# A Restormer block on one core: bands of 16 rows instead of 12, the fourth channel block of every band split by rows between VectorE and TensorE, one pool of sixteen buffers, and an order read from a table of places

## The chip, the core and the metric

The kernel runs on one core of one Trainium2 chip. The metric is device time in microseconds (us), the median of several runs. The core's engines work side by side, each on its own queue of instructions in program order: TensorE (PE, with its weight loads as PEld), VectorE (DVE), ScalarE (ACT), GpSimd (POOL) and SyncE (SP, which only issues transfers). Sixteen DMA engines move data for all of them. An engine that reaches an instruction whose operands are not there waits, and everything behind it on that queue waits too.

## The reference

The input is 16 images of 128 channels and 96x96 pixels, f32. Of each image:

```python
xn1 = _layernorm(x_hwc, ln1_w, ln1_b)            # over the 128 channels of a pixel
attn_out = _attention(xn1, wq, wk, wv, wp)       # 8 heads; channels attend to channels, 16 x 16 a head
x = x + attn_out.transpose(0, 3, 1, 2)
xn2 = _layernorm(x_hwc, ln2_w, ln2_b).transpose(0, 3, 1, 2)
x = x + _ffn(xn2, w_in, w_dw, w_out)
# _ffn: h1 = 1x1 convolution 128 -> 512; h2 = depthwise 3x3 of h1, padding 1;
#       h3 = gelu(h2); 1x1 convolution 512 -> 128
```

## The kernel before

The 128 channels lie on the partitions. An image goes through a first normalisation (names with `_a`), a gram matrix and the attention, which end in one 128x128 matrix for the image (`mats`); then that matrix times the normalised pixels is added to x (`mix`, `mixed`, `add_x`), a second normalisation (names with `_b`) writes the ring `xn`, and the feed-forward part reads the ring. The normalisation of the next image runs beside the convolutions of this one. In a normalisation PE transposes four tiles of 128 pixels into a bank of PSUM, DVE takes statistics (`BATCH_NORM_STATS2`, L876), POOL makes the reciprocal root (L881, L885) and, in the first normalisation, scales the pixels (L909).

The feed-forward part is cut into bands of `BR = 12` rows and four blocks of 128 hidden channels (`NCH = 4`). A band and a block are one job (`conv_job`):

1. `hidden` (PE, L1162) makes the hidden rows in PSUM, 4 or 5 at a time, and `kept` (ACT, L1167) copies them into the padded tile `h1s[n]`. The two rows that a band shares with the one before are copied by `halo` (ACT, L1158).
2. Of the nine taps of the depthwise convolution, ACT multiplies two, three or four out (`product`, L1178, into tiles `pr`). Weights are divided by that of the centre tap, so that the centre needs no product.
3. POOL adds the first product to the centre tap (`merge`, L1181, into the one tile `merged`) and, where there is a fourth product, adds that (`merge_too`, L1184).
4. DVE adds the other taps one after another (`tap`): the first reads `merged` and writes the accumulator `acc` in PSUM (L1190), the middle ones add into `acc` (L1194), the last writes the job's tile `h3` (L1190 again, `h<-h,ratio,acc`). Each of them needs the one before.
5. Transfers issued by POOL add the rest: `add_products` (L1203) the third product into the second, `add_h3` (L1206) the second into `h3`. `gelu` (ACT, L1211) then works in place on `h3`.

The fourth block (`PE_CHUNK`) of a third of the bands (`PE_BANDS`: 10 of every 30, and others in the last image) is instead convolved by PE itself (`by_matmuls`, L1274: nine matmuls for each unit of `UR = 4` rows, and one for the edges, L1280). When the four blocks of a band are done, `ffn_out` multiplies them unit by unit with the output weights (PE, L1315), DVE adds the result to x (L1322), and SP stores the band.

The buffers are pools of their own: `XB_BUFS = 5` bands of x, `PR_BUFS = 8` products, `H3_BUFS = 8` tiles of h3, one `merged`, all of 12 rows, and `X1_BUFS = 2` bands of x for the first normalisation. Four banks of PSUM (`H_BANKS`) serve all that PE writes outside `acc` and the gram matrix.

The order of all this is made by `Plan`: every piece of work is given an engine, a duration, a place (`AT`, `RANK`, and `SHIFTS` for each stretch of the work), its reads and its writes. `Plan.order` plays the engines through in time with these durations: an engine that is free takes the ready work with the lowest place. It also books the time in which POOL and DVE may not read two SBUF tiles at once (`two`, `held`). The program is emitted in the order of the starts that come out.

Of the kernel before, what the change touches and what calls it, by code (L numbers as in the profile page):

```python
# [18 lines left out]
BR = 12  # L19
PE_CHUNK = 3  # L20
PE_BANDS = (0, 3, 6, 9, 12, 15, 18, 21, 24, 27)
PE_OF = 30
PE_LAST = (0, 1, 3, 4, 6)
# [8 lines left out]
FOURTHS = ((0, 1, (0,)),)  # L32
FOURTH_TAP = 6
LAST_TAP, TOP_LAST, END_LAST = 8, 6, 2
RING = 132
# [7 lines left out]
X1_BUFS = 2  # L43
XB_BUFS = 5
PR_BUFS = 8
H3_BUFS = 8
ZT_BUFS = 4
BATCHES = 8
DIRECT = False
IN_TURN = ("zT", "tr", "h3", "pr", "xb", "x1")  # L50
AT = dict(
    load_w=-385.3, weights=-616.15, zeros=-141.7, load_a=-42.4, forth_a=-588.2, stats_a=1671.35, variance_a=269.75,
    power_a=-755.3, pool_product=152.05, merge=-380.8, scaled_a=-1419.9, gram=1191.75, back_a=416.05,
    place_a=228.35, attention=-37, mix=1454.35, residual=-779.15, mixed=-33.8, add_x=-342.3, forth_b=1585.15,
    stats_b=614.45, variance_b=-1160.25, power_b=-1398.6, shift_b=20.9, scaled_b=-3615.05, back_b=417.3,
    place_b=-902.15, halo=4531.85, hidden=416.95, kept=-903.15, products=3487.6, add_last=-380.1, tap=10.85,
    add_first=-1420.85, gelu=4569.5, conv=1192.9, conv_gelu=10.15, out=421.1, add=612.75, store=75.2,
    mix_0=-440.15, residual_0=-785.8, mixed_0=-1036.75, add_x_0=-1518.55, gram_0=475.45, forth_a_0=-103.4,
    forth_b_0=-946.85, stats_a_0=-789.15, stats_b_0=-710.05, scaled_a_0=-915.5, copied_a=35.4, copied_b=-38.35,
    copied_a_0=-43.45, copied_b_0=1111, scaled_b_0=-128.2, back_a_0=485, back_b_0=-1340.55, place_a_0=-547.95,  # L60
    place_b_0=-708.95, shift_b_0=22.8, late=-293.55, load_a_0=-390.35, load_dw=-378, units=-654.05,
    variance_a_0=-172.3, power_a_0=-183.6, variance_b_0=-303.2, power_b_0=-128.75,
)
RANK = dict(tap=-1882.15, products=-1879.1, forth_a=-433, forth_b=-526, conv_gelu=-1389, mix=-1794.75)
STRETCH = 15
SHIFTS = {
    0: dict(load_w=1.9, zeros=-8.4, load_a=-22.8, forth_a=-1.1, stats_a=-0.3, variance_a=-0.3, power_a=-8.1,
        merge=-300.7, gram=0.2, back_a=-0.2, place_a=-1660.1, attention=-276.4, mix=-21.7, residual=-23.2,
        mixed=530.5, forth_b=40.5, stats_b=-118.7, variance_b=14.1, power_b=605.1, back_b=0.1, place_b=1.6,
        halo=4.3, kept=986.6, products=-7.1, add_last=329.8, tap=-1.6, add_first=1.7, gelu=7.1, conv=-6,  # L70
        conv_gelu=0.4, out=0.2, add=-660.9, store=1.7, mix_0=-899, residual_0=-622, gram_0=0.9, forth_a_0=18.5,
        stats_a_0=-2.4, stats_b_0=19.6, scaled_a_0=-65.5, copied_a=-60.9, back_a_0=-6.5, back_b_0=0.2,
        place_a_0=399.7, place_b_0=1296.2, late=10.6, load_a_0=4.4, load_dw=229.6, units=8.6, variance_a_0=619.5,
        power_a_0=-469.8, variance_b_0=-341, power_b_0=-17.1),
    1: dict(load_a=-14.5, forth_a=0.1, stats_a=14.8, variance_a=1354, power_a=1176.9, merge=637, scaled_a=46.3,
# [124 lines left out]
    31: dict(merge=4987, hidden=741.3, kept=1.8, products=1119.8, tap=1184.1, add_first=2628.9, gelu=-4553.7,  # L200
        conv=9, conv_gelu=-2.6, out=4185.8, add=-1517.3, store=4532.1),
}
STEP = dict(scaled=0.3, hidden=0.1, products=0.5, tap=0.166, conv=1.6, conv_tap=0.03, out=0.8, out_part=0.05)
SLACK = 150
LATE = 400
NORM1_END = 6.0
# [1193 lines left out]
```

## Time and profile before

| what | value |
|---|---|
| median of 3 runs | 3966.26 us (3965.86 to 3970.24) |
| span of the profiled execution | 3974.3 us, 0.2% above the median; no other time of it is given |
| PE busy | 3892.4 us, 98% of the span |
| DVE busy | 3834.8 us, 96% |
| ACT busy | 3558.1 us, 90% |
| POOL busy | 3379.4 us, 85% |
| DMA moved | 777.42 MB, 196 GB/s over the span |

The busy time of an engine is the time in which at least one of its instructions is under way; an instruction can begin a little before the one ahead of it ends, so busy time is less than the sum of the durations. In a group of instructions the numbers behind the bar are the busy time in us, the mean of one in ns, and the idle time of the engine just ahead of them with what ended most of it. Rows of the timeline give the start and the length of a run of equal instructions, both in us.

### The profile page before, as it was taken

The page shows a single profiled execution, that of the slowest core. Times are in us where ns is not written, and L with a number is a line of the kernel's source. Part 1 is how long each engine was busy: PE and PEld are TensorE (multiplying, and loading weights), DVE is VectorE, ACT ScalarE, POOL GpSimd, SP SyncE. Part 2 cuts the span into 40 slices and gives each one's busy share as a digit, 9 for nine tenths or more (in the row PEclk, how much of TensorE's full clock was granted, in tenths as well). Part 3 has the DMA queues.
Part 4 walks back from the last instruction along what each step waited for, and adds up shares of the span by engine and source line. Part 5 has one row for each costly group of instructions (what it writes and reads, how often), then busy time and mean ns, then how long its engine had stood idle before and what let it go on. Part 6 is the DMA issues. An engine that isn't in the chain of part 4 may idle for free.

```text
span 3974.3 us, 50973 instructions
## 1 busy us (share of the span) xinstructions
PE 3892.4 (98%) x16760; PEld 2521.7 (63%) x16760; DVE 3834.8 (96%) x4390; ACT 3558.1 (90%) x5186; POOL 3379.4 (85%) x3107
## 2 busy tenths in 40 slices
PE   8999999999999999999999999999999999999999
PEld 7566666666666666666666666666666666665555
DVE  7999999999999999999999999999999999999998
ACT  3989989989999999999989989999899999998886
POOL 5998988898898988988888888888888888888674
PEclk9999999999999999999999999999999999999999
DMA  3999999999999999999999999999999999999996
GB/s 100 187 191 204 200 200 198 199 202 198 210 201 209 203 198 203 200 210 201 194 202 197 207 201 194 205 197 206 189 192 206 203 207 201 203 197 183 191 189 146
DMA packets 191691, 777.42 MB, mean 196 GB/s; under 512 B 22208, under 2 KB 23616, under 8 KB 191424
## 3 DMA queue, kind: packets, MB, share of 16 engines
q0 software_dynamic: 151920, 622.33, 82.6%
q1 hardware_dynamic: 38784, 151.75, 10.2%
q8 instruction: 132, 2.16, 0.2%
q14 instruction: 135, 1.11, 0.1%
q10 hardware_dynamic: 720, 0.07, 0.0%
HBM read 148.85 MB, written 75.50 MB: 56 GB/s over the span
## 4 chain that ended last, share of the span: by engine, by line
PE 58%; DVE 14%; ACT 10%; DMA 7%; POOL 6%; issue 5%; POOLq 0%; DVEq 0%; ACTq 0%
PE h L1315 15%; PE h L1162 14%; PE h L1274 13%; DVE acc L1194 6%; DMA h<-pr 5%; ACT pr L1178 5%; PE h L818 4%; PE h L964 4%; PE g L916 3%; PE h L868 3%; DVE acc L1190 3%; DVE h L1190 2%; ACT h L1167 2%; POOL merged L1181 2%; DMA pr<-pr 2%
## 5 line engine op out<-in xcount | busy, mean ns | idle before, releaser
L1178 ACT ACTIVATE pr<-h,ratio 128x1152 f32<-128x1152 f32 x1494 | 1837.2, 1271 | 37.6 <-DMA h<-pr 12.6
L1194 DVE SCALAR_TENSOR_TENSOR acc<-h,ratio,acc 128x1152 f32<-128x1152 f32 (+1 forms) x1308 | 1810.3, 1384 | 7.7
L1181 POOL TENSOR_TENSOR merged<-pr,h 128x1152 f32<-128x1152 f32 x466 | 1238.1, 2657 | 100.5 <-DVE acc L1190 54.7
L1162 PE MATMUL h<-xn,winT 128*128 128x384 f32 (+2 forms) x2802 | 1088.0, 496 | 16.0 <-ACT h L1167 9.2
L1315 PE MATMUL h<-h,woutT 128*128 128x384 f32 x3072 | 1086.2, 488 | 1.7 <-ACT h L1167 1.1
L1274 PE MATMUL h<-xn,comp 128*128 128x380 f32 (+2 forms) x2430 | 895.0, 482 | 2.2 <-ACT h L1167 1.5
L1167 ACT COPY h<-h 128x384 f32<-128x384 f32 (+2 forms) x1401 | 652.9, 493 | 192.4 <-PE h L1162 187.5
L1315 PEld LDWEIGHTS h<-h,woutT 128*128 128x128 f32 x3072 | 565.2, 190 | 359.3 <-ACT h L1167 7.8
L1162 PEld LDWEIGHTS h<-xn,winT 128*128 128x128 f32 x2802 | 500.0, 190 | 326.6 <-issue 34.2
L1190 DVE SCALAR_TENSOR_TENSOR acc<-h,ratio,merged 128x1152 f32<-128x1152 f32 x466 | 686.6, 1473 | 20.9 <-POOL merged L1184 10.1
L1206 POOL DMA_DIRECT2D h<-pr x466 | 463.3, 994 | 241.9 <-DVE h L1190 57.5
L1190 DVE SCALAR_TENSOR_TENSOR h<-h,ratio,acc 128x1152 f32<-128x1152 f32 x467 | 655.2, 1403 | 3.4
L1211 ACT ACTIVATE h<-h,ksum 128x1152 f32<-128x1152 f32 (+2 forms) x586 | 616.0, 1081 | 46.4 <-DMA h<-pr 45.6
L1274 PEld LDWEIGHTS h<-xn,comp 128*128 128x128 f32 x2430 | 430.6, 189 | 235.2 <-issue 17.1
L1203 POOL DMA_DIRECT2D pr<-pr x466 | 478.7, 1040 | 103.1 <-ACT pr L1178 73.4
L885 POOL TENSOR_TENSOR ve_b<-ve_b,mhalf 128x4 f32<-128x4 f32 x288 | 366.0, 1277 | 7.9
L909 POOL TENSOR_TENSOR zT<-zT,ve_a 128x512 f32<-128x512 f32 x270 | 331.3, 1232 | 8.6
L885 POOL TENSOR_TENSOR ve_a<-ve_a,mhalf 128x4 f32<-128x4 f32 x288 | 318.6, 1109 | 15.3
L868 PE MATMUL h<-ident,x 128*128 128x128 f32 x2244 | 317.0, 275 | 13.7 <-ACT xn L970 4.9
L868 PEld LDWEIGHTS h<-ident,x 128*128 128x128 f32 x2244 | 263.6, 142 | 96.4 <-issue 38.6
L818 PE MATMUL h<-xn,mwT 128*128 128x384 f32 x768 | 289.1, 490 | 7.7 <-ACT h L1167 3.2
L916 PEld LDWEIGHTS g<-zT 128*128 128x128 f32 x2160 | 269.9, 191 | 40.2 <-POOL zT L909 11.0
(190 smaller groups left out, 3967.0 us busy)
## 6 DMA issues: line engine op xcount, KB each, us to landing
pr<-pr POOLq DMA_DIRECT2D x466, 576.0 KB, 7.8
h<-pr POOLq DMA_DIRECT2D x466, 576.0 KB, 7.7
x<-in_x_dram SPq DMA_DIRECT2D x128, 576.0 KB, 7.5
out_dram<-x SPq DMA_DIRECT2D x127, 576.0 KB, 4.6
x<-in_x_dram POOLq DMA_DIRECT2D x123, 576.0 KB, 9.1
out_dram<-x SPq DMA_DIRECT2D x3, 192.0 KB, 1.9
h<-in_L_conv_w_in_dram SPq DMA_DIRECT2D x1, 256.0 KB, 3.4
h<-in_L_conv_w_out_dram SPq DMA_DIRECT2D x1, 256.0 KB, 3.6
```

The costliest lines, as they stand in the source:

```text
L868: nc.tensor.transpose(d["pT", q][:, k, :], xt[:, j * P : (j + 1) * P], ident)
L885: nc.gpsimd.tensor_tensor(rstd, rstd, mhalf, ALU.pow)
L1162: nc.tensor.matmul(rows(ph), lhsT=winT[:, n, :], rhs=window(xn, r0 + r, e - r, 1), start=True, stop=True)
L1167: nc.scalar.copy(window(h1_, r, e - r, 1), rows(d.pop(("ph", r))))
L1178: nc.scalar.activation(to, shifted(t), AF.Copy, scale=ratio[:, n, t : t + 1])
L1181: nc.gpsimd.tensor_tensor(merged, d["pr", dma_taps[0]], shifted(UNIT), ALU.add)
L1190: nc.vector.scalar_tensor_tensor(to, shifted(t), ratio[:, n, t : t + 1], also, ALU.mult, ALU.add)
L1194: nc.vector.scalar_tensor_tensor(to, shifted(t)[:, lo:hi, cut], ratio[:, n, t : t + 1], to, ALU.mult, ALU.add)
L1203: nc.gpsimd.dma_start(out=d["pr", dma_taps[1]], in_=d["pr", t], accum_op=ALU.add)
L1211: nc.scalar.activation(h3, h3, AF.Gelu, bias=ksum[:, z, n : n + 1])
L1274: nc.tensor.matmul(d["pc"][:, lo:hi, cut], lhsT=comp[:, t, :], rhs=window(xn, r0 + dy, UR, dx)[:, lo:hi, cut], start=(t == order[0]), stop ...
L1315: nc.tensor.matmul(rows(d["po"]), lhsT=woutT[:, n, :], rhs=h3s[g, n][:, s * UR : (s + 1) * UR, :], start=(k == 0), stop=(k == NCH - 1),)
```

## The change

- `BR` becomes 16: six bands an image instead of eight, 24 jobs an image instead of about 29. A whole tap is 128x1536 instead of 128x1152, and `acc` fills its three banks.
- The fourth block of every band is split: PE convolves the last unit of 4 rows of the band (`PE_UNITS = 1`; two or three units in the bands of the last image, `PE_LAST`), and a job of the remaining 12 rows goes the way of the other blocks. That job makes all its hidden rows itself and has no `halo`.
- A fourth product is taken in blocks 0 and 2 of every band and in block 1 of every second one (`FOURTHS`), but not in the first and the last band of an image; before only in block 0.
- `merge` adds in place into the product's own tile; the tile `merged` is gone.
- x, products and h3 share `BUFS = 16` tiles of 16 rows. The first normalisation loads x in pieces of `XR = 8` rows into three small tiles.
- `ffn_out` works on `OC = 512` columns instead of 384: three pieces a band, each with an add and, in the last band, a store.
- `Plan.op` takes neither engine nor duration. Each piece of work has a place from the table `PLACES`: one for the first image, one that is repeated for images 1 to 14 with `PERIOD` added for each, one for the last. `Plan.order` emits the ready work with the lowest place for which a buffer is free; nothing is played through in time, and `two` and `held` are gone.

```diff
-BR = 12
+BR = 16
+XR = 8
+OC = 512
 PE_CHUNK = 3
-PE_BANDS = (0, 3, 6, 9, 12, 15, 18, 21, 24, 27)
-PE_OF = 30
-PE_LAST = (0, 1, 3, 4, 6)
+PE_UNITS = 1
+PE_LAST = (2, 2, 2, 2, 2, 3)
...
-FOURTHS = ((0, 1, (0,)),)
+FOURTHS = ((0, 1, (0,)), (2, 1, (0,)), (1, 2, (0,)))
...
-X1_BUFS = 2
-XB_BUFS = 5
-PR_BUFS = 8
-H3_BUFS = 8
-ZT_BUFS = 4
+X1_BUFS = 3
+XB_FIRST = 4
+BUFS = 16
+ZT_BUFS = 3
...
+PERIOD = 2533.91
+PLACES = (
...
+        tap=(862.03, 886.3, 688.92, 919.54, 935.53, 955.22, 974.9, 995.58, 1012.83, 1030.39, 1045.8, 1136.89,
...
 class Plan:
...
+        if kind:
+            n = self.count[kind] = self.count.get(kind, -1) + 1
+            self.place = self.at + PLACES[self.era][kind][n]
+        self.ops.append((self.place, list(needs), new, work))
...
+        while ready:
+            place, k = heapq.heappop(ready)
+            new = ops[k][2]
+            pools = [t[0] for t in new]
+            lacks = [p for p in pools if len(free[p]) < pools.count(p)]
+            if lacks:
+                waiting[lacks[0]].append(k)
+                continue
+            for t in new:
+                self.slot[t] = free[t[0]].pop(0)
+            order.append(k)
...
-    merged = h1p.tile([P, BR, W], F32, name="merged")
-    pr_bufs = [h1p.tile([P, BR, W], F32, name=f"pr_{k}") for k in range(PR_BUFS)]
-    h3_bufs = [h1p.tile([P, BR, W], F32, name=f"h3_{k}") for k in range(H3_BUFS)]
+    bufs = [h1p.tile([P, BR, W], F32, name=f"buf_{k}") for k in range(BUFS)]
...
     def conv_job(j, g, n):
...
-        from_halo = b > 0 and (n != PE_CHUNK or not by_pe(g - 1))
-        to_halo = b < NB - 1 and (n != PE_CHUNK or not by_pe(g + 1))
+        R = BR if n != PE_CHUNK else BR - UR * pe_units(g)
+        whole = R == BR
+        top, bottom = b == 0, b == NB - 1 and whole
+        from_halo, to_halo = b > 0 and whole, b < NB - 1 and whole
...
         def merge():
-            nc.gpsimd.tensor_tensor(merged, d["pr", dma_taps[0]], shifted(UNIT), ALU.add)
+            nc.gpsimd.tensor_tensor(d["pr", dma_taps[0]], d["pr", dma_taps[0]], shifted(UNIT), ALU.add)
 
         def merge_too():
-            nc.gpsimd.tensor_tensor(merged, merged, d["pr", dma_taps[3]], ALU.add)
+            nc.gpsimd.tensor_tensor(d["pr", dma_taps[0]], d["pr", dma_taps[0]], d["pr", dma_taps[3]], ALU.add)
...
-    def ffn_out(p, g, s):
+    def ffn_out(g, s):
...
             nc.tensor.matmul(
-                rows(d["po"]), lhsT=woutT[:, n, :], rhs=h3s[g, n][:, s * UR : (s + 1) * UR, :],
-                start=(k == 0), stop=(k == NCH - 1),
+                d["po"], lhsT=woutT[:, n, :], rhs=flat(h3s[g, n])[:, cols], start=(k == 0), stop=(k == NCH - 1)
             )
...
+    def pe_units(g):
+        i, b = divmod(g, NB)
+        return PE_LAST[b] if i == B - 1 else PE_UNITS
```

The order on DVE, in the middle of the program (the second job of a band). In the names `h_0_141` to `h_3_144` are the padded hidden tiles of the four blocks before, and `h_0_157` to `h_3_160` those after, `h_73` to `h_76` the four banks, `zT` the transposed pixels, `buf` the common tiles. Before:

```order
L1190 SCALAR_TENSOR_TENSOR acc<-h_1_142,ratio,merged 128x1152
L876 BN_STATS st_a_5_13366<-zT_162 128x6
L1194 SCALAR_TENSOR_TENSOR acc<-h_1_142,ratio,acc 128x1056
L968 TENSOR_TENSOR xn<-x_8_0_13009,h_76 128x4x96
L1194 SCALAR_TENSOR_TENSOR acc<-h_1_142,ratio,acc 128x1056
L968 TENSOR_TENSOR xn<-x_8_1_13223,h_73 128x4x96
L1194 SCALAR_TENSOR_TENSOR acc<-h_1_142,ratio,acc 128x1056
L968 TENSOR_TENSOR xn<-x_8_1_13223,h_74 128x4x96
L1190 SCALAR_TENSOR_TENSOR h_2_156<-h_1_142,ratio,acc 128x1152
```

And the same engine after, about the middle of its program too (the end of a band and the first job of the next):

```order
L1275 SCALAR_TENSOR_TENSOR acc<-h_3_160,ratio,acc 128x1152
L1271 SCALAR_TENSOR_TENSOR buf_169<-h_3_160,ratio,acc 128x1152
L1271 SCALAR_TENSOR_TENSOR acc<-h_0_157,ratio,buf_162 128x1536
L1275 SCALAR_TENSOR_TENSOR acc<-h_0_157,ratio,acc 128x1536 x2
L1271 SCALAR_TENSOR_TENSOR buf_167<-h_0_157,ratio,acc 128x1536
L948 BN_STATS st_137<-zT_178 128x6 x2
L1271 SCALAR_TENSOR_TENSOR acc<-h_1_158,ratio,buf_166 128x1536
L1275 SCALAR_TENSOR_TENSOR acc<-h_1_158,ratio,acc 128x1536
```

Before, almost every tap has another piece of work between itself and the next tap; after, several taps follow each other directly. Counted over the whole program, a tap stands directly ahead of another tap 374 times among 2,258 before, and 801 times among 1,780 after.

The order on POOL, in the middle of the program: the merges, what stands right behind them, and the issues of the transfers. Before:

```order
L1206 DMA h_1_155<-pr_148 128x1152
L1203 DMA pr_153<-pr_151 128x1152
L1181 TENSOR_TENSOR merged<-pr_146,h_1_142 128x1152
L1206 DMA h_2_156<-pr_147 128x1152
L1203 DMA pr_149<-pr_152 128x1152
L1181 TENSOR_TENSOR merged<-pr_150,h_2_143 128x1152
L881 TENSOR_SCALAR ve_b_2_10268<-st_b_2_10237 128x4
```

After:

```order
L1283 DMA buf_172<-buf_174 128x1536
L1280 DMA buf_171<-buf_161 128x1152
L953 TENSOR_SCALAR ve_140<-st_132 128x4
L957 TENSOR_TENSOR ve_140<-ve_140,mhalf 128x4
L1262 TENSOR_TENSOR buf_168<-buf_168,h_0_157 128x1536
L1265 TENSOR_TENSOR buf_168<-buf_168,buf_169 128x1536
L953 TENSOR_SCALAR ve_145<-st_137 128x4
L1280 DMA buf_176<-buf_170 128x1536
```

Every merge had the tile `merged` as its goal, so that it stood behind the first tap of the job before; now each goes into a tile of its own, and merges of two additions are more frequent (160 second additions among 383 jobs with merges, against 96 among 466). The last merge of a job has a short instruction or an issue behind it nearly everywhere, before and after: another long addition or scaling follows directly 31 times in 464 before and 2 times in 382 after.

911 lines of the change are left out of this document (428 added, 483 removed), and 125 rows, old and new, of tables (conv, hidden, kept, out).

## The prediction

> **What bounds the kernel now.** I read the first part of the page, then the busy time by stretch, then the groups with different shapes apart, then short pieces of the timeline, because on queues this full the step from one start to the next says more than a duration.
>
> ```profile
> span 3974.3 us, 50973 instructions
> ...
> PE 3892.4 (98%) x16760; PEld 2521.7 (63%) x16760; DVE 3834.8 (96%) x4390; ACT 3558.1 (90%) x5186; POOL 3379.4 (85%) x3107
> ...
> DMA packets 191691, 777.42 MB, mean 196 GB/s; under 512 B 22208, under 2 KB 23616, under 8 KB 191424
> ...
> q0 software_dynamic: 151920, 622.33, 82.6%
> q1 hardware_dynamic: 38784, 151.75, 10.2%
> ```
>
> Five resources are nearly full. The stretches (busy us of PE, PEld, DVE, ACT, POOL, then the granted clock, the DMA share and GB/s) say where the idle time lies:
>
> ```profile
> 0.00:100.00 100.00, 90.02 (x596) 73.11 (x597) 72.50 (x186) 35.01 (x73) 55.83 (x113) 1.00 0.34 101
> 700.00:1200.00 500.00, 495.30 (x2172) 322.88 (x2171) 491.05 (x558) 463.74 (x682) 440.42 (x403) 1.00 0.97 203
> 3450.00:3500.00 50.00, 47.37 (x208) 30.58 (x207) 47.11 (x55) 45.56 (x66) 43.53 (x43) 1.00 1.04 224
> 3900.00:3975.00 75.00, 70.77 (x229) 41.50 (x227) 58.80 (x51) 38.75 (x54) 25.33 (x18) 0.99 0.60 132
> ```
>
> In the body PE and DVE are both busy 98 to 99%, ACT 93%, POOL 88%. So PE and DVE bound the kernel together: a gain on one alone is worth nothing. Of the 139.5 us that DVE idles, 27.5 lie in the first 100 us and 16.2 in the last 75; the body holds 95.8, or 2.5%.
>
> **The change, engine by engine.** Instructions and elements are counted from both programs; durations and steps come from these rows.
>
> ```profile
> L1178 ACT ACTIVATE pr<-h,ratio 128x1152 f32<-128x1152 f32 x1494 | 1837.2, 1271 | 37.6 <-DMA h<-pr 12.6 <-DMA pr<-pr 10.0 <-POOL merged L1181 2.2
> L1194 DVE SCALAR_TENSOR_TENSOR acc<-h,ratio,acc 128x1152 f32<-128x1152 f32 x957 | 1349.9, 1411 | 5.3
> L1181 POOL TENSOR_TENSOR merged<-pr,h 128x1152 f32<-128x1152 f32 x466 | 1238.1, 2657 | 100.5 <-DVE acc L1190 54.7 <-ACT pr L1178 28.6 <-ACT h L1167 5.1
> L1315 PE MATMUL h<-h,woutT 128*128 128x384 f32 x3072 | 1086.2, 488 | 1.7 <-ACT h L1167 1.1 <-ACT h L1211 0.2
> L1190 DVE SCALAR_TENSOR_TENSOR acc<-h,ratio,merged 128x1152 f32<-128x1152 f32 x466 | 686.6, 1473 | 20.9 <-POOL merged L1184 10.1 <-POOL merged L1181 4.2 <-DVE h L1190 0.5
> L1190 DVE SCALAR_TENSOR_TENSOR h<-h,ratio,acc 128x1152 f32<-128x1152 f32 x467 | 655.2, 1403 | 3.4
> L1167 ACT COPY h<-h 128x384 f32<-128x384 f32 x1092 | 506.8, 488 | 144.8 <-PE h L1162 142.0
> L1203 POOL DMA_DIRECT2D pr<-pr x466 | 478.7, 1040 | 103.1 <-ACT pr L1178 73.4 <-ACT h L1158 11.0 <-ACT x L827 3.6
> L1194 DVE SCALAR_TENSOR_TENSOR acc<-h,ratio,acc 128x1056 f32<-128x1056 f32 x351 | 460.4, 1312 | 2.3
> L909 POOL TENSOR_TENSOR zT<-zT,ve_a 128x512 f32<-128x512 f32 x270 | 331.3, 1232 | 8.6
> L1322 DVE TENSOR_TENSOR x<-h,x 128x384 f32<-128x384 f32 x384 | 211.6, 551 | 39.3 <-PE h L1315 31.6 <-ACT pr L1178 3.2 <-issue 1.7
> L1167 ACT COPY h<-h 128x480 f32<-128x480 f32 x192 | 105.7, 566 | 33.5 <-PE h L1162 31.6 <-DVE xn L968 1.5
> L1280 PE MATMUL h<-ident,edgeT 6*128 6x8 f32 x248 | 47.6, 262 | 0.0
> ```
>
> ```profile
> 1510.79 1.40 DVE L1194 SCALAR_TENSOR_TENSOR acc<-h,ratio,acc 128x1152 f32<-128x1152 f32 x1
> 1512.10 0.42 DVE L876 BATCH_NORM_STATS2 st_a<-zT 128x6 f32<-128x256 f32 x1
> 1512.44 2.86 DVE L1194 SCALAR_TENSOR_TENSOR acc<-h,ratio,acc 128x1152 f32<-128x1152 f32 x2
> ```
>
> ```profile
> 1513.45 4.03 PE L1315 MATMUL h<-h,woutT 128*128 128x384 f32 x12
> ```
>
> ```profile
> 1514.08 3.55 ACT L1178 ACTIVATE pr<-h,ratio 128x1152 f32<-128x1152 f32 x3
> ```
>
> ```profile
> 1502.26 0.88 POOL L1203 DMA_DIRECT2D pr<-pr  x1
> 1502.86 1.36 POOL L885 TENSOR_TENSOR ve_b<-ve_b,mhalf 128x4 f32<-128x4 f32 x1
> ```
>
> *DVE.* From 1056 to 1152 elements a tap grows by 99 ns, 1.03 ns an element, which leaves 0.224 us fixed in 1.411. But the fixed part depends on what follows. At 1510.79 the statistics behind a tap start 1.31 us after it, 0.10 before its mean length is over. Of the two taps in one run, 2.86 us long, the second starts 2.86 - 1.40 = 1.46 us after the first, since it needs the first one's result. A tap directly ahead of a tap so costs 0.15 us more. The change takes 478 instructions of this kind away (478 x 0.124 = 59 us) and 74,208 elements (76 us), and makes 427 more direct successions (+64 us). The adds are 96 fewer for the same elements: their fixed part is 0.551 - 384 x 0.00103 = 0.155 us, of which I count 0.1, 10 us. Sum: -59 - 76 + 64 - 10 = **-81 us**.
>
> *PE.* Twelve records of 384 columns took 4.03 us; less the last one's 0.49 this is 0.322 us a step, 0.84 ns a column. The convolution loses 576 records (-185 us), the edges 54 (at 47.6 / 248 = 0.19, -10). The twelve-row jobs make their overlapping rows again: 21,984 more columns in two passes, +37. The output has as many columns as before. Sum: **-158 us**, so that PE keeps 77 us of room that DVE lacks.
>
> *ACT.* Three products in 3.55 us: the step is (3.55 - 1.27) / 2 = 1.14 us. From 384 to 480 elements a copy grows by 78 ns, 0.81 ns an element; 0.207 us of a product's step is fixed. More fourth products and fewer, longer instructions: +173,952 elements (+141), 303 fewer ACTIVATEs (-63), 102 fewer copies at 0.05 us of fixed step and 3,552 fewer elements (-8): **+70 us**. Hidden as long as ACT stays below DVE: 3628 busy us in a span near 3890 are 93%, where it has 90% now.
>
> *POOL.* 2657 - 1232 ns over 640 elements are 2.23 ns an element; 148,224 more give +330. 197 fewer issues give back 0.60 us each by the step at 1502.26, 1.03 by the row's busy time: -118 to -203. Net **+127 to +212**, 90 to 92% of the new span. Against that, the 54.7 us in which the merge waited for the first tap of the job before are gone with the tile `merged`; late next is the product from ACT (28.6).
>
> *DMA.* Software-queue bytes go from 622.33 to 635.4 MB. At 0.826 x 3974 / 622.33 = 5.27 us a MB this is **+69 us** of all sixteen engines, with the other queue 3757 in all, 97% of the new span, where it is 93% now; 790.5 MB in 3885 us are 203 GB/s. The body runs at 203 for 500 us and at 224 in the fullest 50 us shown, so this still fits. SP has 286 issues for 258 and waits for nothing that others need.
>
> *Start and end.* The same steps stand there; the first load grows from 576 to 768 KB, under a microsecond by the 7.5 us to landing of the group below. I count nothing.
>
> *Sum.* DVE ends last in the body after the change, as PE leaves more room than it. Its idle time can shrink, because PE relieves it and the merge's wait goes, or grow, because ACT, POOL and DMA come closer to full and four banks serve longer instructions. No row prices this: the lower bound is half of the body's 96 us gone (-48), the upper one that ACT's rise shows through whole (+70). I take zero, between the ends and nearest to what the body shows now with two full engines. So the span is 3974.3 - 81 = 3893. The profiled execution lies 8.0 us over the median; against the median this is 3966 - 81 = **3885 us**.
>
> [...]
>
> **The rivals.**
>
> 1. *The order of the taps costs nothing.* If the 0.15 us are only where the wait shows, and the engine gets them back, DVE saves 198 us. For it: half of the new idle could be filled by work that has slipped. Against it: the step of 1.46 is idle on the engine itself. 3966 - 198 = 3768, with PE's -158 then as the limit: 3808 at best.
> 2. *Idle time shrinks too.* PE falls behind DVE, so that DVE no longer waits for it: 31.6 of 39.3 us before L1322 are PE's. Half of the body's idle gone: 3885 - 48 = 3837.
> 3. *ACT takes the gain.* Its copies free the banks that PE writes; if ACT's +70 shows whole, 3955. Against it: ACT idles 416 us, and 187.5 of it waits for PE, which gets faster.
> 4. *Slower: the adding transfers land late.* These rows give transfers (KB, us to landing) and ACT's waits for them (total, times, longest):
>
> ```profile
> pr<-pr POOLq DMA_DIRECT2D x466, 576.0 KB, 7.8
> h<-pr POOLq DMA_DIRECT2D x466, 576.0 KB, 7.7
> x<-in_x_dram SPq DMA_DIRECT2D x128, 576.0 KB, 7.5
> ```
>
> ```profile
> ACT h L1167 <- PE h L1162: 187.5, 242, 9.5
> ACT h L1211 <- DMA h<-pr: 45.6, 37, 4.9
> ```
>
>    A third more bytes make the 7.7 us 10.3, 2.6 more. Behind the gelu that waits stand ACT's copies, and PE waits for those. Now 37 of 466 jobs wait. If one job in six of 383 (64) waits 2.6 us more, 166 us are lost: 3885 + 166 = 4051, or about 4010 if ACT's slack takes a quarter. It decides from 81 / 2.6 = 31 such waits. For it: DMA at 97%. Against it: the common buffers let products run further ahead.
> 5. *Slower: the first tap waits for POOL's merges.* The first tap reads two SBUF tiles and takes 1473 ns, 70 more than the last one of the same size. A whole merge of two additions is now near 2 x 3.5 us, and if 100 of 383 first taps met one and waited half an addition, 175 us were lost: 4060. It decides from 81 / 1.75 = 46. The order speaks against it: behind the last merge a short instruction or an issue stands in 380 of 382 places. The Trainium skill's page "SBUF — State Buffer", section "Who interferes with whom", says that a DVE instruction with two SBUF inputs and a GpSimd one that reads SBUF share a read port, and whoever issues first holds it for the whole instruction; the 70 ns agree with a rare wait of this kind.
> 6. *The table does not do what it says:* the new order loses as much as the work saves, 3966.
>
> **How the numbers follow.** The forecast gets 0.42 (own range 3860 to 3912), rival 1 0.06, rival 2 0.20, rival 3 0.15, rival 4 0.09, rival 5 0.04, rival 6 0.04. The measurement can tell 0.2%, 8 us, from no change. Faster: forecast, 1, 2 and most of 3 (0.12), 0.80. Same: 6 and the rest of 3, 0.07. Slower: 4 and 5, 0.13. The range goes from 3800, below rivals 2 and 1's limit, to 3990, which takes in rival 3 and the near end of 4; about 2 in 10 stay outside, mostly above.
>
> **What the profile after would show.** The whole middle tap at 128x1536 takes 1.78 to 1.84 us; a run of two is 0.05 us longer than twice that, and an instruction of another kind starts about 0.1 us before a tap ends. DVE busy is near 3740, PE near 3740, ACT near 3630, POOL 3500 to 3590; DVE, not PE, has the least idle time in the body. The product takes 1.55 to 1.60 us, the merge 3.4 to 3.6. The forecast is wrong if DVE's idle time in the body is above 180 us (then the rows of ACT's waits for `DMA buf<-buf`, or of the first tap, say whether 4 or 5 holds), or if taps in a row take no more than others.

## The result, and the profile after

The changed kernel takes 4103.24 us (median of 4 runs, 4091.67 to 4107.38) where the kernel before takes 3968.25 (3965.86 to 3974.8): ratio 1.0334, 95% interval 1.0316 to 1.0352. It is 3.3% slower; 3885 was predicted, and a range that ended at 3990.

The head of the page of the changed kernel, in the same rows as before:

```profile
span 4098.8 us, 46552 instructions
PE 3841.7 (94%) x15428; PEld 2286.8 (56%) x15428; DVE 3746.5 (91%) x3816; ACT 3657.3 (89%) x4781; POOL 3559.4 (87%) x2890
DMA packets 167329, 790.29 MB, mean 193 GB/s; under 512 B 19504, under 2 KB 20528, under 8 KB 167088
q0 software_dynamic: 123552, 635.49, 80.3%
```

The work is what it should be: DVE has 88 us less to do. But DVE now idles 4098.8 - 3746.5 = 352.3 us, where it idled 139.5. That is 213 us more, against 88 saved; 213 - 88 = 125 is the difference of the two spans. The stretches (PE, PEld, DVE, ACT, POOL busy, clock, DMA share, GB/s) show that it is lost everywhere, not at the ends:

```profile
700.00:1200.00 500.00, 473.52 (x1906) 281.94 (x1905) 462.56 (x465) 459.18 (x602) 447.43 (x361) 0.98 0.94 199
3200.00:3700.00 500.00, 472.02 (x1904) 281.68 (x1903) 462.28 (x464) 458.05 (x602) 448.30 (x361) 0.98 0.93 198
```

In the body PE is busy 94.5%, DVE 92.5%, ACT 92%, POOL 89.5%, the DMA engines 93.5%. Before, two engines stood at 98 to 99%. Now nobody is full: five queues wait for each other. The chain that ended last says the same (before first, then after):

```profile
PE 58%; DVE 14%; ACT 10%; DMA 7%; POOL 6%; issue 5%; POOLq 0%; DVEq 0%; ACTq 0%
```

```profile
PE 29%; POOL 27%; DMA 13%; ACT 11%; DVE 10%; issue 7%; POOLq 0%; DVEq 0%; ACTq 0%
```

It ran on PE for more than half of the time; now it hands over between PE and POOL. What DVE waited for (line, waited for: us in total, times, longest), after:

```profile
DVE acc L1271 <- POOL buf L1265: 119.8, 85, 3.5
DVE buf L1394 <- PE h L1388: 42.6, 34, 5.0
DVE buf L1271 <- DMA buf<-buf: 33.0, 25, 3.3
```

The largest is the first tap of a job (L1271) that waits for POOL's second merge (L1265): 119.8 us, where the same wait took 10.1 us before (the group L1190 in the prediction). A look at one of them, in the timeline (start, us, engine, line), DVE and then POOL:

```profile
937.93 1.81 DVE L1271 SCALAR_TENSOR_TENSOR buf<-h,ratio,acc 128x1536 f32<-128x1536 f32 x1
943.20 1.82 DVE L1271 SCALAR_TENSOR_TENSOR acc<-h,ratio,buf 128x1536 f32<-128x1536 f32 x1 [3.46 <-POOL buf L1265]
```

```profile
932.71 3.83 POOL L1262 TENSOR_TENSOR buf<-buf,h 128x1536 f32<-128x1536 f32 x1
935.85 1.67 POOL L957 TENSOR_TENSOR ve<-ve,mhalf 128x4 f32<-128x4 f32 x1
937.60 1.04 POOL L981 TENSOR_TENSOR zT<-zT,ve 128x512 f32<-128x512 f32 x1
938.61 0.19 POOL L953 TENSOR_SCALAR ve<-st 128x4 f32<-128x4 f32 x1
938.74 0.93 POOL L901 DMA_DIRECT2D buf<-in_x_dram  x1
939.43 3.74 POOL L1265 TENSOR_TENSOR buf<-buf,buf 128x1536 f32<-128x1536 f32 x1
```

POOL ends the first merge at 936.5 and starts the second at 939.4. Between them it does a power, a scaling, a variance and the issue of a transfer, because the table has put them there. DVE, whose next instruction is the first tap, stands still from 939.7 to 943.2. The same first tap waits 2.4 to 3.5 us at 439, 690, 940, 1191, 1440, 1947, 2197 us and on to 3711, 13 times, nearly always 250 us apart: one set of places serves images 1 to 14, and what it loses once it loses in nearly every image.

A second loss of this kind lies on PE. `a`, the last step of the attention on DVE, stands once an image; its 16 instructions took 15.6 us before and take 35.4 now, and PE waits for them (2.6 us before):

```profile
L1182 DVE TENSOR_SCALAR a<-em,rden 128x128 f32<-128x128 f32 x16 | 35.4, 2211 | 0.6
```

```profile
PE g L1186 <- DVE a L1182: 32.5, 14, 3.4
```

What makes them long is told with run 8 and in the last section.

### The profile page after: what moved, and what is told of

Read it like the earlier page. It is cut to its first block, busy times and chain, and to the rows that moved or that the text cites. A ratio compares the mean times of both kernels' runs of the same rounds, so it can differ in the third digit from the quotient of the medians.

```text
span 4098.8 us, 46552 instructions
## 1 busy us (share of the span) xinstructions
PE 3841.7 (94%) x15428; PEld 2286.8 (56%) x15428; DVE 3746.5 (91%) x3816; ACT 3657.3 (89%) x4781; POOL 3559.4 (87%) x2890
## 3 DMA queue, kind: packets, MB, share of 16 engines
q0 software_dynamic: 123552, 635.49, 80.3%
## 4 chain that ended last, share of the span: by engine, by line
PE 29%; POOL 27%; DMA 13%; ACT 11%; DVE 10%; issue 7%; POOLq 0%; DVEq 0%; ACTq 0%
DMA buf<-buf 10%; PE h L1388 8%; PE h L1243 8%; POOL buf L1262 8%; ACT buf L1259 7%; POOL ve L957 6%; PE h L1349 4%; DVE acc L1275 4%; POOL buf L1265 4%; POOL zT L981 3%; POOL buf L1280 3%; PE h L889 2%; DMA buf<-in_x_dram 2%; DVE acc L1271 2%; PE h L1036 2%
## 5 line engine op out<-in xcount | busy, mean ns | idle before, releaser
L1259 ACT ACTIVATE buf<-h,ratio 128x1536 f32<-128x1536 f32 (+2 forms) x1309 | 1931.2, 1508 | 66.7 <-DMA buf<-buf 51.4
L1275 DVE SCALAR_TENSOR_TENSOR acc<-h,ratio,acc 128x1536 f32<-128x1536 f32 (+5 forms) x995 | 1647.2, 1655 | 18.6
L1262 POOL TENSOR_TENSOR buf<-buf,h 128x1536 f32<-128x1536 f32 x383 | 1231.4, 3215 | 62.5 <-ACT buf L1259 58.5
L1243 PE MATMUL h<-xn,winT 128*128 128x384 f32 (+1 forms) x2868 | 1155.5, 512 | 59.0 <-ACT h L1248 39.3
L1388 PE MATMUL h<-buf,woutT 128*128 128x512 f32 x2304 | 1077.5, 600 | 6.6 <-ACT buf L1288 4.7
L1248 ACT COPY h<-h 128x384 f32<-128x384 f32 (+3 forms) x1434 | 671.4, 497 | 155.4 <-PE h L1243 148.2
L1271 DVE SCALAR_TENSOR_TENSOR acc<-h,ratio,buf 128x1536 f32<-128x1536 f32 x383 | 665.6, 1738 | 134.2 <-POOL buf L1265 119.8
L957 POOL TENSOR_TENSOR ve<-ve,mhalf 128x4 f32<-128x4 f32 x576 | 677.1, 1176 | 35.5
L1271 DVE SCALAR_TENSOR_TENSOR buf<-h,ratio,acc 128x1536 f32<-128x1536 f32 (+2 forms) x384 | 653.0, 1701 | 42.2 <-DMA buf<-buf 33.0
L1349 PE MATMUL h<-xn,comp 128*128 128x380 f32 (+3 forms) x1854 | 655.3, 483 | 0.7 <-ACT h L1248 0.7
L1288 ACT ACTIVATE buf<-buf,ksum 128x1536 f32<-128x1536 f32 (+6 forms) x496 | 597.6, 1228 | 22.7 <-DMA buf<-buf 22.2
L1265 POOL TENSOR_TENSOR buf<-buf,buf 128x1536 f32<-128x1536 f32 x160 | 565.0, 3531 | 27.2 <-ACT buf L1259 17.7
L1283 POOL DMA_DIRECT2D buf<-buf x383 | 387.6, 1012 | 154.5 <-DVE buf L1271 73.1
L1280 POOL DMA_DIRECT2D buf<-buf x383 | 382.3, 998 | 99.1 <-ACT buf L1259 77.0
```

The lines of the kernel that those rows point to most:

```text
L957: nc.gpsimd.tensor_tensor(rstd, rstd, mhalf, ALU.pow)
L1243: nc.tensor.matmul(rows(ph), lhsT=winT[:, n, :], rhs=window(xn, r0 + r, e - r, 1), start=True, stop=True)
L1248: nc.scalar.copy(window(h1_, r, e - r, 1), rows(d.pop(("ph", r))))
L1259: nc.scalar.activation(to, shifted(t), AF.Copy, scale=ratio[:, n, t : t + 1])
L1262: nc.gpsimd.tensor_tensor(d["pr", dma_taps[0]], d["pr", dma_taps[0]], shifted(UNIT), ALU.add)
L1265: nc.gpsimd.tensor_tensor(d["pr", dma_taps[0]], d["pr", dma_taps[0]], d["pr", dma_taps[3]], ALU.add)
```

## The experiments

The theories, as the expectations name them. A: the lost time is the first tap's wait for the second merge. A2: POOL and ACT have no slack left with so many fourth products, whatever the order. B: the order that the table gives, which nothing at run time can correct, leaves the engines waiting; the same work in another order would take another time. C: sixteen common buffers are too few. Times are medians; the kernel before ran beside them on the same chip (3969 to 3970 us); the changed kernel's 4103.24 is from the section above. Lines are those of the changed kernel but for three runs, whose code above them is longer or shorter: in runs 2 and 3 a line's number is up to 6 higher, in run 5 it is 235 lower. Runs 7 and 10 have the lines of the kernel before.

**1. The second merge out of the first tap's way.** `merge_too` adds the fourth product to another product:

```diff
-            nc.gpsimd.tensor_tensor(d["pr", dma_taps[0]], d["pr", dma_taps[0]], d["pr", dma_taps[3]], ALU.add)
+            nc.gpsimd.tensor_tensor(d["pr", dma_taps[1]], d["pr", dma_taps[1]], d["pr", dma_taps[3]], ALU.add)
...
-                op("merge", merge_too, [pr[3]], [pr[0]])
+                op("merge", merge_too, [pr[3]], [pr[1]])
```

> The second merge adds the fourth product into the product that the transfers collect (tap 5's) in place of the one that the first tap reads, so no tap waits for it; all work is the same. Theory A (the lost time is the first tap's wait for POOL's second merge, 119.8 us in 85 waits): that wait falls under 30 us, DVE's idle time from 352 to some 250, time 4000 us (3980 to 4040). Theory B (the fixed order paces the kernel at about its own period, and what one wait gives back the next takes): 4085 to 4120 us. Theory C (the common buffers are too few): within 0.3% of 4103, with the waits for a buffer (33 us of DVE, 51 us of ACT) unchanged or longer.

Measured: 4769.69 us, 16% slower than the changed kernel. No theory expected it. The waits of POOL name the reason:

```profile
POOL buf L1265 <- ACT buf L1259: 514.1, 125, 12.8
```

The second merge needs no first merge any more, so the table's place for it now holds by itself; where it is an early one (in 63 of the 160 jobs the second merge now stands ahead of the first), the merge stands at the head of POOL's queue before ACT has made the product, and everything behind it on POOL waits up to 12.8 us. The removed wait could not be tried alone: with the order kept, the second merge would in 77 of the 160 jobs stand ahead of the product that it adds to. The run says nothing on A, but it was the first sign that a place in the order costs more than the work at it.

**2. The second merge made short**, on one row of the tile instead of all.

```diff
-            nc.gpsimd.tensor_tensor(d["pr", dma_taps[0]], d["pr", dma_taps[0]], d["pr", dma_taps[3]], ALU.add)
+            nc.gpsimd.tensor_tensor(
+                d["pr", dma_taps[0]][:, :1, :], d["pr", dma_taps[0]][:, :1, :], d["pr", dma_taps[3]][:, :1, :], ALU.add
+            )
```

> The second merge adds one of the 16 rows only (15 rows of the fourth product are left out of the sum), so POOL loses about 160 x 3.3 = 530 us of its 3559 us. Theory A: the first tap's wait for it falls under 15 us; 3970 to 4010 us. Theory A2 (all of POOL's queue is late, the power and the scaling of the normalisations too, 89.8 + 42.0 + 47.1 + 27.5 us on PE): these fall as well, 3880 to 3960 us. Theory B (the order): over 4060 us. Theory C (buffers): 4050 to 4100 us.

Measured: 4022.37 us, 81 less than the changed kernel.

```profile
span 4016.8 us, 46578 instructions
PE 3811.1 (95%) x15428; PEld 2275.4 (57%) x15428; DVE 3718.1 (93%) x3816; ACT 3646.8 (91%) x4781; POOL 3074.0 (77%) x2890
```

POOL has 485 us less to do and falls to 77%. The first tap's wait for L1265 is no longer among the longest, but DVE still idles 4016.8 - 3718.1 = 298.7 us. The span fell by 82: 54 of it is DVE's idle time, less than half of the 119.8 us that it had waited there, and 28 is its busy time. That is `a` again: with the merges short, its row falls from 35.4 us to 4.6, and PE's wait for it from 32.5 to 1.4.

```profile
L1182 DVE TENSOR_SCALAR a<-em,rden 128x128 f32<-128x128 f32 x16 | 4.6, 289 | 0.6
```

The time lies between the ranges of A and A2 and that of B. So in this order all that the long second merge does, A, A2 and its part in `a` together, explains at most 81 of the 135 us between the two kernels; the rest stays with POOL at 77%. PE's waits for the power are an example (weight loads that wait for L957, 89.8 us in the changed kernel, here):

```profile
PEld h L1036 <- POOL ve L957: 85.3, 80, 2.4
```

**3. Fourth products only in block 0, all other work at its place.**

```diff
-FOURTHS = ((0, 1, (0,)), (2, 1, (0,)), (1, 2, (0,)))
+FOURTHS = ((0, 1, (0,)),)
...
-            op("tap", lambda t=t: tap(t), r, w)
+            op(None if placed and t == FOURTH_TAP else "tap", lambda t=t: tap(t), r, w)
```

(`placed` marks the jobs that lost their fourth product; the places of the two operations that are gone are skipped, and the tap that comes back stands behind the tap before it.)

> Only block 0 keeps its fourth product (64 of 160 left): 96 taps more on VectorE (96 x 1.82 = +175 us), 96 products less on ScalarE (-152 us), 96 merges less on POOL (-339 us); all else keeps its place in the order. DVE busy 3921 us. Theory A: the wait for the second merge falls with their number, by 72 us: DVE idle 280, time 4200 us. Theory A2 (POOL and ACT have no slack left, the whole idle time is theirs): idle back to some 140 to 180: 4060 to 4110 us. Theory B (the order paces it, waits stay): 4250 us and more.

Measured: 4147.50 us.

```profile
PE 3855.8 (93%) x15428; PEld 2288.6 (55%) x15428; DVE 3895.2 (94%) x3912; ACT 3534.0 (85%) x4685; POOL 3227.2 (78%) x2794
```

DVE's busy time rose by 149 us, and in a span of 4146.2 us its idle time fell by 101, to 251. With POOL at 78% and ACT at 85% there is slack on both, and DVE still idles 112 us more than before the change. No range held: idle time fell by more than A expected (72) and by less than A2 (to 140 to 180), and B's 4250 was too slow. So the load of POOL and ACT has a part in the idle time, but not the whole of it. The run also answers whether the fourth products were too many for DVE's sake: taking 96 of them back costs, in this order, more than it frees.

**4. Fifteen buffers.** `BUFS = 15`.

> Fifteen common buffers in place of sixteen, all else the same. Theory C (buffers): the waits for a buffer double (84 us of DVE and ACT to 170) and the time rises by over 1%, to 4145 us and more. Theories A and B: within 0.5% (4083 to 4125 us).

Measured: 4442.08 us, 339 us or 8% slower.

```profile
ACT buf L1259 <- DMA buf<-buf: 240.2, 171, 3.3
```

ACT's wait for a free buffer goes from 51.4 to 240.2 us. By itself this looks like C. But one buffer less also changes the order: an operation that finds no buffer is passed over, and what comes after it is emitted first. So it does not separate C from B. A seventeenth buffer does not fit into the memory, so the other direction was not tried; how much more than the 51.4 + 33.0 us of ACT's and DVE's waits for transfers the number of buffers costs stays open.

**5 and 6. The same work in another order.** Run 5 has other numbers in `PLACES`, found by small moves (see its expectation), with 2533.21 for `PERIOD`; run 6 has one other number:

```diff
-PERIOD = 2533.91
+PERIOD = 2540
```

> The same instructions, buffers and dependences as the changed kernel; only the numbers of the table of places are other ones, so each engine issues the same work in another order (found by trying small moves of the places one after the other and keeping those after which the engines, by the durations of the trace, would wait less). Theory B (the idle time belongs to the order that the table gives, not to the work or to the sixteen buffers): 3960 us (3920 to 4010), DVE's idle time from 352 us to 180 to 260, all busy times unchanged within 1%. Theory A2 (POOL and ACT have no slack with this work) and theory C (the buffers are too few): any order of this work loses about as much, 4060 us and more.

> One number of the table is changed: the step from one image's places to the next is 2540 in place of 2533.91 (0.24% more), so that now and then an operation of one image changes places with one of the next. No instruction, size or buffer changes. Theory B (the order sets the time and is cut very closely): 4250 to 4500 us, with waits on all engines. Theories A2 and C (work or buffers set it): 4103 within 1% (4060 to 4145).

Measured: run 5 takes 4029.17 us, 74 less than the changed kernel (ratio to before 1.0152, 1.0135 to 1.0169). Run 6 takes 4434.21 us, 331 more. Busy time and the first tap's wait of run 5, then of run 6:

```profile
span 4025.7 us, 46608 instructions
PE 3824.9 (95%) x15428; PEld 2284.3 (57%) x15428; DVE 3725.6 (93%) x3816; ACT 3661.3 (91%) x4781; POOL 3532.0 (88%) x2890
```

```profile
DVE acc L1036 <- POOL buf L1030: 82.4, 105, 2.6
```

```profile
PE 3953.2 (89%) x15428; PEld 2337.8 (53%) x15428; DVE 3773.4 (85%) x3816; ACT 3670.4 (83%) x4781; POOL 3577.5 (81%) x2890
```

```profile
DVE acc L1271 <- POOL buf L1265: 115.3, 85, 3.2
```

All three kernels issue the same instructions on the same sixteen buffers; each engine's count is the same in the three rows. They differ by 405 us. So B holds in so far as the same work takes another time in another order, and a period that is 0.24% longer costs four times what the whole change should have gained. In run 5 the first tap's wait is 82.4 us for 119.8, and PE's wait for `a` has gone from 32.5 us to 0.3; of its gain, 52 us are DVE's idle time and 21 its busy time, in which `a`'s row falls from 35.4 to 6.6 us. Run 6 is also against A: the first tap's wait is 115.3 us in 85 times, as before, while the time is 331 us longer. Run 5 missed its forecast of 3960 and its bound of 4010: 300 us of DVE's idle time are left, and whether they belong to the order as well this run does not show.

**7. One part of the change alone.** The kernel before, with its 12 rows and its planner, gets the three blocks of fourth products.

```diff
-FOURTHS = ((0, 1, (0,)),)
+FOURTHS = ((0, 1, (0,)), (2, 1, (0,)), (1, 2, (0,)))
```

> The kernel before (12 rows, its own buffers, order worked out by its planner's clock) with the changed kernel's three blocks of fourth products: 240 jobs of 12 rows instead of 96. DVE loses 144 taps of 1.42 us (-204 us), ACT gains 144 products of 1.27 us (+183), POOL 144 merges of 2.66 us (+383, to 3760 us). The prediction's way of counting (DVE and PE bind, the rest hides): PE's 3892 us stay, 3950 to 3990 us. Theory A2 (POOL without slack loses time, whatever the order): 4050 us and more. Theory B (an order not fitted to the new work loses time): over 4100 us, and the idle time is spread over all engines instead of sitting at the second merge.

Measured: 4306.17 us (1.085, 1.0834 to 1.0866).

```profile
PE 4016.4 (93%) x16760; PEld 2543.1 (59%) x16760; DVE 3691.6 (86%) x4246; ACT 3732.9 (87%) x5330; POOL 3786.8 (88%) x3251
```

```profile
DVE acc L1190 <- POOL merged L1184: 193.8, 127, 4.2
DVE x L1322 <- PE h L1315: 153.3, 97, 5.5
```

My way of counting fails here as it did for the change: DVE's work falls by 143 us and the time rises by 337. The planner's clock has the new work, its places and corrections were set for the old. It doesn't tell A2 from B by itself, since POOL rose to 3787 us.

**8. A longer search.** The places of run 5 were searched further (`PERIOD` is 2533.61):

> Again the same instructions, buffers and dependences as the changed kernel and another set of places, searched for longer and with transfers and instructions that vary a little, as they do on the chip. Theory B (the idle time belongs to the order): 3995 us (3960 to 4020), DVE idle under 280 us. Theories A2 and C (work or buffers keep the rest): the first new order has got what there was, 4020 to 4050 us.

Measured: 4075.34 us, 28 less than the changed kernel but 46 more than run 5. All theories missed: a place that looks good by durations taken from a trace is not good when a duration depends on the place. One row points to it. It is that of `a`, for which PE waits (its duration in ns: shortest, median, longest; its first and last start); run 5, then run 8:

```profile
L947 DVE TENSOR_SCALAR a<-em,rden x16: 285/288/1969, 64.9 to 3709.0; 128x128 f32<-128x128 f32 x16
```

```profile
L1182 DVE TENSOR_SCALAR a<-em,rden x16: 288/3230/4336, 65.2 to 3757.1; 128x128 f32<-128x128 f32 x16
```

The same instruction on 128x128 elements takes 0.29 us or 3.2, by what stands beside it. DVE's idle time is the same in the two runs (300.1 and 300.8 us); its busy time is 47 us longer in run 8 (3773.0 for 3725.6), and 45 of these are `a` (51.4 us in all for 6.6). That is as much as the 46 by which run 8 lies above run 5. That it is the cause of the 46 is inferred: no run changed `a`'s place alone.

**9 and 11. Fewer fourth products, and then the order alone.** Both leave the 32 fourth products of block 1 out (128 instead of 160) and DVE takes those taps. Run 9 has places that were searched for this work (with 2531.96 for `PERIOD`), run 11 the table's own places, without those of the operations that are gone and with one for the tap that comes back.

```diff
-FOURTHS = ((0, 1, (0,)), (2, 1, (0,)), (1, 2, (0,)))
+FOURTHS = ((0, 1, (0,)), (2, 1, (0,)))
```

> The changed kernel without the fourth products of block 1 (128 of 160 left), with places searched for this work in the same way. DVE gets 32 taps back (+58 us), POOL loses 32 merges (-113 us), ACT 32 products (-51 us). Theory B with A2 (an order can hide the less, the nearer POOL and ACT are to full): 3965 us (3935 to 3995), DVE's idle time 170 us or less with 3790 busy. Theory B alone (only the order matters, POOL's load does not): DVE's 58 us show, 4040 us and more.

> The work of run r9 (no fourth products in block 1) with the changed kernel's own places instead of the searched ones; the 32 taps that come back stand behind the tap before them. Theory B (in r9 the order made most of the gain): 4085 us (4050 to 4115), so that order alone is worth about 100 us on this work. Theory A2 (the 32 merges and products fewer made it): 4000 us (3980 to 4030).

Measured: run 9 takes 3983.25 us (ratio to before 1.0029, 1.0018 to 1.0039), run 11 takes 4059.62 (1.0229, 1.0212 to 1.0246). Run 9, then run 11:

```profile
PE 3794.9 (95%) x15428; PEld 2267.3 (57%) x15428; DVE 3772.0 (95%) x3848; ACT 3625.6 (91%) x4749; POOL 3418.4 (86%) x2858
```

```profile
PE 3838.0 (95%) x15428; PEld 2280.2 (56%) x15428; DVE 3781.8 (93%) x3848; ACT 3612.0 (89%) x4749; POOL 3447.7 (85%) x2858
```

The instructions of the two are the same in number on every engine. So the way from the changed kernel to run 9 is 44 us of work taken off ACT and POOL (4103 to 4060) and 76 us of order alone (4060 to 3983). The 76 repeat the 74 of run 5 on other work. Run 11 lies in B's range and not in A2's; the 44 show that less work on POOL and ACT counts too, if less than the order. Run 9 came 18 us above its forecast and idles 209 us on DVE, not 170.

**10. The kernel before without its corrections.** The planner of before has a table of its own, `SHIFTS`, which moves the places for each stretch of the work:

```diff
-        return Place(place + (AT[of] + SHIFTS.get(max(0, int(place // STRETCH)), {}).get(of, 0)), RANK.get(kind, 0))
+        return Place(place + (AT[of] + 0), RANK.get(kind, 0))
```

> The kernel before with the same planner, but without its table of corrections by stretch (SHIFTS counts as zero): the same instructions and buffers, another order, still played through in time. Theory B (an order costs what it was not fitted for, here less, because the planner's clock never lets an engine wait for a piece of work while another is ready): 4010 us (3985 to 4060). Theories A2 and C (work or buffers set the time): 3968 us within 0.3%.

Measured: 4035.14 us (1.0166, 1.015 to 1.0181), 65 slower, with the same counts as before.

```profile
PE 3919.2 (97%) x16760; PEld 2524.7 (63%) x16760; DVE 3840.5 (95%) x4390; ACT 3564.6 (88%) x5186; POOL 3379.4 (84%) x3107
```

```profile
DVE x L1322 <- PE h L1315: 52.3, 47, 3.9
```

This is in B's range. So the kernel before owes part of its low idle time (139.5 on DVE) to its order: with the corrections gone, the same work idles 4033.8 - 3840.5 = 193.3, and PE is waited for longer (31.6 before).

**12. A search that keeps `a` short.** Run 9's work; the places were searched further (`PERIOD` is 2534.01), and those that put `a` beside POOL's merges were avoided.

> The work of run r9 with places searched further, now with the port of `a` (attention on VectorE against POOL's merges) and more variation of transfers taken into account. Theory B: 3972 us (3955 to 3985), no measurable difference from the kernel before. If what is left of the idle time belongs to the work (A2): 3983 us as r9, or more.

Measured: 3974.82 us, against 3969.67 of the kernel before beside it: ratio 1.001, 1.000 to 1.002.

```profile
span 3974.5 us, 46537 instructions
PE 3785.6 (95%) x15428; PEld 2272.1 (57%) x15428; DVE 3766.7 (95%) x3848; ACT 3622.0 (91%) x4749; POOL 3409.7 (86%) x2858
```

```profile
DVE acc L1271 <- POOL buf L1265: 43.8, 56, 2.9
```

```profile
L1182 DVE TENSOR_SCALAR a<-em,rden x16: 285/286/361, 63.0 to 3661.5; 128x128 f32<-128x128 f32 x16
```

`a` now takes 0.29 us in every image but for one of 0.36, and the first tap's wait has fallen from 119.8 us to 43.8. This is the best of the changed kernels: 128 us under the table's own, with 32 fourth products fewer, and within what can be told from the kernel before. It has the same sixteen buffers, so for this work they are enough to come that near. DVE still idles 207.8 us, 68 more than before, which eat the 68 us that its work has shrunk by (3834.8 to 3766.7). No version beat the kernel before; whether any order of the changed work does stays open.

## Why the prediction was wrong, step by step

The work was counted right, in these groups of the changed kernel (behind the bar: busy us, mean ns, idle us just ahead of the group and what ended it):

```profile
L1259 ACT ACTIVATE buf<-h,ratio 128x1536 f32<-128x1536 f32 x1024 | 1579.0, 1580 | 36.4 <-DMA buf<-buf 24.3 <-PE h L1388 4.4
L1262 POOL TENSOR_TENSOR buf<-buf,h 128x1536 f32<-128x1536 f32 x288 | 985.4, 3421 | 52.0 <-ACT buf L1259 48.0 <-DVE acc L1275 1.4
L1275 DVE SCALAR_TENSOR_TENSOR acc<-h,ratio,acc 128x1536 f32<-128x1536 f32 x416 | 756.8, 1819 | 9.0
L1265 POOL TENSOR_TENSOR buf<-buf,buf 128x1536 f32<-128x1536 f32 x160 | 565.0, 3531 | 27.2 <-ACT buf L1259 17.7 <-DMA buf<-buf 0.6
L1271 DVE SCALAR_TENSOR_TENSOR acc<-h,ratio,buf 128x1536 f32<-128x1536 f32 x288 | 532.8, 1850 | 132.0 <-POOL buf L1265 119.8 <-POOL buf L1262 8.1 <-DVE buf L1271 0.5
```

- *DVE, -81.* Right, if closer than the sum deserves: 3834.8 to 3746.5 is -88, but `a`, which the sum has at nothing, grew by 20 (15.6 to 35.4), so that the rest fell by 108. The middle tap takes 1819 ns (1.78 to 1.84 forecast). The two rules on successors hold as well, in the timeline:

```profile
1501.42 1.41 DVE L1271 SCALAR_TENSOR_TENSOR buf<-h,ratio,acc 128x1152 f32<-128x1152 f32 x1
1502.74 0.76 DVE L948 BATCH_NORM_STATS2 st<-h 128x6 f32<-128x256 f32 x2
...
1506.96 3.68 DVE L1275 SCALAR_TENSOR_TENSOR acc<-h,ratio,acc 128x1536 f32<-128x1536 f32 x2
```

  The statistics start 0.09 us before the tap ends (0.1 forecast), and a run of two takes 3.68, 0.04 more than twice 1.82 (0.05 forecast).
- *PE, -158.* Mis-sized: busy time fell by 51 only, to 3841.7 (3740 forecast). The step per column was right, in this run of eight matmuls:

```profile
1521.14 3.59 PE L1388 MATMUL h<-buf,woutT 128*128 128x512 f32 x8
```

  (3.59 - 0.60) / 7 = 0.43 us for 512 columns, 0.84 ns a column as before (0.60 is the mean of one such matmul in its group). The count of columns is the same in the changed kernel and its other orders, but these 15,428 records are busy 3785.6 us in run 12 and 4017.6 in run 1. The mean granted clock of the two spans differs; this is run 1:

```profile
PE 4017.6 (84%) x15428; PEld 2387.1 (50%) x15428; DVE 3818.0 (80%) x3816; ACT 3689.2 (77%) x4781; POOL 3566.4 (75%) x2890
core 0: 4772.5 us, clock 0.938
```

  The clock is 0.938 there, with PE 84% busy; it is 0.965 in run 6 (89%), 0.986 in the changed kernel (94%), 0.995 in run 12 (95%) and 0.998 before (98%). From run 12 to run 1 the clock alone gives 3785.6 x 0.995 / 0.938 = 4016. So in these runs a PE that waited more also worked more slowly. The Trainium skill's page "TensorE: Matmul & The Clock Gate", section "What's actually happening", says that the clock is set by how busy PE has been in a short window; these means agree in direction. The clock is not the whole: scaled in the same way from run 12, it gives 3903 of the 3953 us of run 6 and 3820 of the 3842 of the changed kernel, and run 12 itself, at nearly the clock of before, is 107 us below before and not 158. The rest is not explained.
- *ACT, +70.* Somewhat low: 3558.1 to 3657.3 is +99. The product's 1580 ns lie in the range.
- *POOL, +127 to +212.* Right: +180, at 3559.4. The merges take 3421 and 3531 ns (3.4 to 3.6 forecast).
- *DMA, +69.* Mis-sized. The bytes are right (635.49 MB for 635.4), but the time of this queue's packets rose from 0.826 x 3974.3 = 3283 us to 0.803 x 4098.8 = 3291, by 8: it did not go with the bytes. So the DMA engines are at 93.5% in the body and not at 97, and not only because the span is longer.
- *Start and end, nothing.* Right: what was lost lies in the body.
- *Idle time: "I take zero".* This step failed. It was bounded at -48 to +70 and measured at +213. The bounds were made from engines that "come closer to full", as if idle time were a property of the work alone. Runs 5 and 6, and 9 and 11, show that the order sets much of it: equal work, 405 and 76 us apart, of which 364 and 65 are idle time of DVE. Run 10 shows that the 95.8 us in the body before, to which I held mine nearest, were so few because that order was corrected for that kernel: 54 us of idle time come back without the corrections. How the 213 divide is shown in part. Run 5's order takes 52 of them back with all the work in place, and run 12's, with 32 fourth products fewer, 145 (207.8 us are left for 352.3); what of the rest belongs to the order, to POOL and ACT closer to full or to the buffers stays open. I read the places of the new order for what stands next to what, but did not price them with the durations of the trace.
- *Rival 5, 0.04.* This mechanism came, and the chance was too low: 85 waits of 1.41 us on average, where it decided from 46 of 1.75. My argument against it was that a short instruction stands behind the last merge in nearly all places. That speaks of the read port. But the first tap waits for the merge to be done, and there the queue ahead of the merge counts, as the timeline of 932 to 943 us shows. Run 2 sizes it: at most 81 us with all else that the long merge does, `a` among it.
- *Rival 4.* False as it was told: the gelu's waits for transfers fell from 45.6 to 22.2 us, and the larger transfers landed after 7.8 us where 7.7 was seen before (the row follows). But the products wait 51.4 us for transfers on the common buffers where they waited 22.6, and the last tap 33.0 us where its group had idled 3.4 in all; no run prices these alone.

```profile
buf<-buf POOLq DMA_DIRECT2D x576, 768.0 KB, 7.8
```

- *Rivals 1 to 3.* None: DVE's work fell by about what the successions said and not by the 198 us of rival 1 (478 x 0.224 + 76 + 15), DVE's idle time grew, and in run 3 ACT at 85% did not bring the time back.
- *Rival 6, 0.04*, that the order loses what the work saves, was nearest in kind, but the order loses 2.4 times that (213 of 88).
- "DVE, not PE, has the least idle time in the body": false, PE 94.5%, DVE 92.5%. "Wrong if DVE's idle time in the body is above 180": it was, and the rows of the first tap said which rival.

## What to carry to other kernels

When the change replaces what makes the order, and all engines are over 85% busy, the order is a term of the sum of its own: walk a stretch of the new order with the durations of the trace, engine by engine, before writing zero for idle time. Such a walk is no exact forecast: runs 5 and 8, whose orders were found by it, came out 69 and 80 us above what was expected of them, runs 9 and 12 18 and 3. A fixed order carries the durations that it was made with inside it; a change of one size, one buffer or one period can cost more than the work it moves, and what it loses once it can lose in every repeat. To tell work from order, run the same instructions in another order (runs 5, 6, 9 and 11 here) before blaming the longest wait.

## What the runs showed of the hardware

- A small DVE instruction can take ten times its length beside POOL's long additions: `a` takes 0.29 us at its shortest, up to 3.3 in the changed kernel (the rows of runs 5, 8 and 12 are above) and up to 4.34 in run 8. The Trainium skill's page "SBUF — State Buffer", section "Who interferes with whom", says that a `tensor_scalar` can enter a mode that takes the pair of ports shared with GpSimd, and that whoever issues first holds it for the whole instruction. One of the long ones of run 8 beside POOL's work, DVE's row and then POOL's, agrees:

```profile
1015.38 3.22 DVE L1182 TENSOR_SCALAR a<-em,rden 128x128 f32<-128x128 f32 x1
```

```profile
1015.35 3.17 POOL L1262 TENSOR_TENSOR buf<-buf,h 128x1536 f32<-128x1536 f32 x1 [1.01 <-ACT buf L1259]
```

  The merge started 0.03 us ahead and ended at 1018.52; `a` ended 0.08 us later, at 1018.60. In run 12, where the search kept `a` away from the merges, it is short.
- PE's busy time and granted clock went with how much it waited, as said above: 232 us between runs 12 and 1, which issue the same matmuls.
